# Values of a batch's tokens from seven block products in place of eight, in a decoder layer on one core

## The chip, the core and the metric

The kernel runs on one core of a Trainium2 chip, as one program with one launch. The metric is the device time of that program in microseconds: the median of several runs. Of the engines, TensorE (PE in the profile, its weight loads PEld) multiplies matrices, VectorE (DVE), ScalarE (ACT) and GpSimd (POOL) work element by element, and SyncE (SP) issues most of the DMAs. Each engine works through a queue of its own in a fixed order. [...]

## The reference

A decoder layer in fp32 over 16 batches of 256 tokens with 256 features. Each of three parts is added to its input and layer-normed.

```python
x = layernorm(x + recurrent(x))              # in-projection, causal convolution, 16-state scan, out-projection
x = layernorm(x + cross_attention(ctx, x))   # 8 heads of 128
x = layernorm(x + experts(x))                # 8 experts, top 2, capacity 512 tokens each
```

The second part matters here. Its keys and values come from the 77 normed context rows and from the 256 normed tokens of the same batch (333 rows in all), its queries from the tokens:

```python
xn = _layernorm(ctx, gamma_media, beta_media)
ln = _layernorm(x, gamma_lat, beta_lat)
q = ln @ Wq + bq
kv = concatenate([xn, ln], axis=1) @ Wkv + bkv
k, v = split(kv, 2, axis=-1)
out = softmax(q k^T * DH**-0.5) v            # per head
return out @ Wo + bo
```

The values of a batch's tokens, before the bias, are a matrix of 256 tokens by 1024 columns: the product of a 256 x 256 matrix (tokens by features) with a 256 x 1024 matrix (the right half of `Wkv`).

## The kernel before

**Stages.** A prologue runs the recurrent part for the first pair of batches and makes the normed context (`context`), its values for all batches (stored in DRAM as `vc`) and everything that batch 0 needs. Then comes the head loop: 16 batches x 8 heads. It ends at about 1066 us, and the experts follow to the end at 1230 us.

**The head loop.** Iteration i issues `head_kq` of head i (keys `pk`, queries `pq`), then extra steps that hang on this head, then `head_out` of head i-2 (values times probabilities, `po`), `head_softmax` of head i (scores `s` on TensorE; `nm` on DVE, exponentials on ACT, `rs` and `pn` on DVE) and `head_turn` of head i-1 (transposes `pa`, `pb`, copied to `ptt`).

**The extra steps.** A dictionary `steps`, filled through `at(b, h, f, ...)`, says which piece of other work stands at which head of which batch: finishing batch b-1 (`project` with `pw`, `turn_tokens`, `score_experts` with `pl`, `choose`, `dispatch`, `settle`) and preparing batch nb = b+1. Even batches prepare an odd one and also run the in-projections (`rec_in`, `ph`) of the next pair at heads 4 to 7; odd batches prepare an even one, with `rec_state` and `rec_out` first. Preparing a batch means `prep_norm` (`zl`), `prep_keys` (the transposed normed tokens `kvt`, one half of the features at a time) and `prep_values`.

**The values.** `prep_values(b, n)` is called for n = 0 to 3, at heads 4, 5, 6, 7 of odd batches and 1, 4, 5, 6 of even ones. Call n takes one block of 128 tokens (`jc`) and one half of the 1024 columns (`half`): two products with 128 features each, accumulated in one bank `pv`, which DVE (half 0) or ACT (half 1) copies into `vs[b]`. Call 0 also issues the DMA that brings the context's values (`v<-vc`). A matmul of fp32 numbers that is written once appears in the trace as two instructions.

**Banks.** `pk`, `pq`, `pa`, `po` have a bank each and `s` two. The remaining two have the tag `mm` and serve all extra steps, the values among them.

**Order.** The program framework (`TileContext`) places waits by itself, and for each engine makes the order in which its instructions are put into its queue when the program is built: among instructions that it thinks ready, by its own estimates of costs, the one written first. Once built, the order of a queue is fixed.

Of the kernel before, what the change touches and what calls it, by code (L numbers as in the profile page):

```python
# [10 lines left out]
F32 = mybir.dt.float32  # L11
I32 = mybir.dt.int32
AF = mybir.ActivationFunctionType
ALU = mybir.AluOpType
# [4 lines left out]
P = 128  # L19
# [9 lines left out]
INNER = H * DH  # L29
E, FI, CAP = 8, 512, N // 8  # L30
DC = D // P
# [7 lines left out]
def decoder_layer(  # L39
# [29 lines left out]
    V, A, G, T = nc.vector, nc.scalar, nc.gpsimd, nc.tensor  # L69
# [14 lines left out]
    def bank(name, tag="mm", bufs=2):  # L84
        return ps.tile([P, 512], F32, tag=tag, bufs=bufs, name=name)
# [79 lines left out]
    wpool = work.enter_context(tc.tile_pool(name="wB", bufs=1))  # L165
# [5 lines left out]
    wkv_s = wpool.tile([P, DC, 2 * INNER], F32, tag="wkv", name="wkv_s")  # L171
# [6 lines left out]
    gl = wpool.tile([P, DC], F32, tag="gl", name="gl")  # L178
    bl = wpool.tile([P, DC], F32, tag="bl", name="bl")
    emb_s = wpool.tile([P, DC, E], F32, tag="emb", name="emb_s")  # L180

    kvc = wpool.tile([P, DC, B * M], F32, tag="kvc", name="kvc")

    b2 = work.enter_context(tc.tile_pool(name="b2", bufs=2))
    b1 = work.enter_context(tc.tile_pool(name="b1", bufs=1))
# [27 lines left out]
    for t0, t1 in ((0, 1), (1, 5), (5, NCT - 1), (NCT - 1, NCT)):  # L213
        c = b2.tile([P, t1 - t0, D], F32, tag="v" if t1 - t0 == 4 else "ctx", name=f"ctx{t0}")
# [104 lines left out]
    def rec_out(b):  # L319

        pr, i = divmod(b, PB)
        py = bank(f"py{b}")
        for h in range(2):
            c0 = i * S + h * P
            T.matmul(py[:, h * D : (h + 1) * D], lhsT=yss[pr][:, c0 : c0 + P], rhs=outw, start=True, stop=True)
        y = b2.tile([P, 2, D], F32, tag="ya", name=f"ya{b}")
        V.tensor_tensor(
            y.rearrange("p h d -> p (h d)"),
            py,
            xts.pop(b).rearrange("p h d -> p (h d)"),  # L330
            ALU.add,
        )
        xs[b] = xpool.tile([P, 2, DX], F32, tag="xs", name=f"xs{b}")
        stats[b] = layernorm(xs[b], y, 2, P, f"a{b}")
        if b + 2 < B:
            load_x(b + 2)
# [3 lines left out]
    zs, kvts, vs, outs_t = {}, {}, {}, {}  # L340
# [47 lines left out]
    def prep_keys(b):  # L388
# [12 lines left out]
            )  # L401
        kvts[b] = kvt

    def prep_values(b, n):

        if n == 0:
            vs[b] = b2.tile([P, 3, INNER], F32, tag="v", name=f"v{b}")
            nc.sync.dma_start(vs[b][0:M, 2, :], vc_d[b * M : (b + 1) * M, :])
        jc, half = divmod(n, 2)
        pv = bank(f"pv{b}_{n}")  # L410
        f0 = half * 512
        for k in range(DC):
            T.matmul(  # L413
                pv,
                lhsT=kvts[b][:, k, jc * P : (jc + 1) * P],
                rhs=wkv_s[:, k, INNER + f0 : INNER + f0 + 512],
                start=(k == 0),
                stop=(k == DC - 1),
            )
        if half == 0:  # L420
            V.tensor_copy(vs[b][:, jc, f0 : f0 + 512], pv)
        else:
            A.copy(vs[b][:, jc, f0 : f0 + 512], pv)

    kts, qts, pns, ptts = {}, {}, {}, {}

    def head_kq(b, h):

# [233 lines left out]
    def at(b, h, f, *args):  # L662
        if 0 <= b < B:
            steps[b, h].append((f, args))
# [4 lines left out]
    for b in range(B):  # L669
        nb = b + 1  # L670
        new_pair = nb % PB == 0 and nb < B
        if b > 0:
            early = int(b == B - 1)
            at(b, 2, project, b - 1, 0)
            at(b, 3, project, b - 1, 1)
            at(b, 5 - early, turn_tokens, b - 1)
            at(b, 6 - early, score_experts, b - 1)
            at(b, 6 - early, choose, b - 1)
            at(b, 7 - early, dispatch, b - 1)
            at(b, 7, settle, b - 1)  # L680
        if new_pair:
            at(b, 0, rec_state, nb // PB)
            at(b, 1, rec_out, nb)
            at(b, 2, prep_norm, nb)
            at(b, 3, rec_out, nb + 1)
            at(b, 3, prep_keys, nb)
            for n, h in enumerate((4, 5, 6, 7)):
                at(b, h, prep_values, nb, n)
        elif nb < B:
            at(b, 0, prep_norm, nb)  # L690
            at(b, 0, prep_keys, nb)
            for n, h in enumerate((1, 4, 5, 6)):
                at(b, h, prep_values, nb, n)
            if nb + 1 < B:
                pr = (nb + 1) // PB
                at(b, 0, load_xT, pr)
                for c in range(NI):
                    at(b, 4 + c, rec_in, pr, c)
# [12 lines left out]
    prep_keys(0)  # L711
    context(4)
    rec_out(1)
    for n in range(4):
        prep_values(0, n)
    for t in range(5, NCT):
        context(t)
# [248 lines left out]
```

## Time and profile before

| | us |
|---|---|
| median of 3 runs | 1229.26 (1229.24 to 1230.31) |
| profiled execution | 1232.08 |
| its span (first to last instruction) | 1230.4 |
| PE busy (matmuls) | 1187.3 (96%) |
| DVE busy | 725.9 (59%) |
| ACT busy | 489.4 (40%) |
| POOL busy | 274.5 (22%) |
| value products of the batches (L413, 256 instructions) | 121.6 busy, of 592 ns each (median) |
| their copies on DVE (L421, 32) | 22.0, of 688 ns each |
| their copies on ACT (L423, 32) | 18.7, of 585 ns each |

How to read it: a line such as `L413 PE MATMUL pv<-wkv_s,kvt` names the source line, the engine, the operation, and the tiles written and read. Durations of matmuls contain the time in which results still drain while the next matmul already streams, so the busy time of neighbours overlaps, and the distance between starts is the better measure of what a matmul costs. In a row of groups the mean duration is followed by the idle time of the engine before it and by what ended it. A timeline row has the start, the time from the first start to the last end, and the number of instructions that follow each other.

### The profile page before, as it was taken

How to read it: one execution, taken by the hardware profiler on the slowest of the kernel's cores; microseconds unless marked ns; L12 is line 12 of the kernel's file. 1: busy time of each engine (PE TensorE's matmuls, PEld its weight loads, DVE VectorE, ACT ScalarE, POOL GpSimd, SP SyncE). 2: the span in 40 equal slices, each digit the busy share in tenths (PEclk: the TensorE clock that was granted, in tenths of full speed). 3: DMA queues.
4: the chain of work that ended last, by engine and by line, in shares of the span. 5: the costliest groups of instructions: out<-in, count | busy, mean ns of one | idle time of the engine just before them, and what ended most of it. 6: DMA issues, size and time to landing. Idle time of an engine off the chain costs nothing.

```text
span 1230.4 us, 15284 instructions
## 1 busy us (share of the span) xinstructions
PE 1187.3 (96%) x5000; PEld 842.3 (68%) x5000; DVE 725.9 (59%) x2122; ACT 489.4 (40%) x1270; POOL 274.5 (22%) x500
## 2 busy tenths in 40 slices
PE   7799999999999999999999999999999999889995
PEld 3356777767776777677767776777677778756663
DVE  6535755684558555756486548564766464555654
ACT  3135434443435344534353434443543344313331
POOL 3200021122111311131111210221021112135566
PEclk9899999999999999999999999999999999999998
DMA  8730100010001100010000000000001000146762
GB/s 262 245 107 1 37 18 29 9 54 18 29 9 32 37 11 20 26 37 5 19 21 28 12 19 19 22 9 14 9 13 43 13 9 3 29 146 147 177 158 82
DMA packets 43617, 60.80 MB, mean 49 GB/s; under 512 B 7945, under 2 KB 31414, under 8 KB 43538
## 3 DMA queue, kind: packets, MB, share of 16 engines
q1 hardware_dynamic: 36674, 50.34, 12.8%
q0 software_dynamic: 6144, 9.48, 3.3%
q8 instruction: 39, 0.64, 0.2%
q14 instruction: 40, 0.33, 0.1%
q10 hardware_dynamic: 720, 0.01, 0.0%
HBM read 36.55 MB, written 30.78 MB: 55 GB/s over the span
## 4 chain that ended last, share of the span: by engine, by line
PE 82%; DVE 7%; POOL 3%; issue 3%; DMA 3%; ACT 1%; POOLq 0%; SPq 0%; DVEq 0%
PE po L484 12%; PE pk L433 10%; PE s L448 10%; PE pw L502 9%; PE pq L438 8%; PE pv L413 8%; PE ph L281 5%; PE pa L471 4%; PE pi L798 3%; PE pvc L365 3%; PE px L301 2%; PE pf L814 2%; PE pb L471 2%; PE pl L544 1%; DMA xe<-xg 1%
## 5 line engine op out<-in xcount | busy, mean ns | idle before, releaser
L450 DVE TENSOR_REDUCE nm<-s 128x2 f32<-128x666 f32 x128 | 108.4, 847 | 144.7 <-PE s L448 144.4
L484 PE MATMUL po<-ptt,v 128*128 128x256 f32 (+1 forms) x768 | 190.2, 382 | 2.2 <-DVE ptt L473 2.2
L484 PEld LDWEIGHTS po<-ptt,v 128*128 128x128 f32 (+1 forms) x768 | 144.2, 191 | 57.1 <-issue 32.7
L433 PE MATMUL pk<-kvt,wkv_s 128*128 128x333 f32 x512 | 165.1, 444 | 0.0
L448 PE MATMUL s<-kt,qt 128*128 128x333 f32 x512 | 164.4, 442 | 0.0
L492 ACT ACTIVATE ot<-po,bkv_s 128x256 f32<-128x256 f32 x128 | 60.6, 474 | 235.4 <-PE po L484 235.3
L454 ACT ACTIVATE p<-s,nm 128x333 f32<-128x333 f32 x256 | 135.1, 534 | 37.9 <-DVE nm L450 28.6
L438 PE MATMUL pq<-kvt,wq_s 128*128 128x256 f32 x512 | 131.2, 379 | 0.0
L413 PE MATMUL pv<-wkv_s,kvt 128*128 128x512 f32 x256 | 121.6, 599 | 0.0
L448 PEld LDWEIGHTS s<-kt,qt 128*128 128x128 f32 x512 | 96.5, 189 | 31.2 <-ACT qt L440 0.5
L438 PEld LDWEIGHTS pq<-kvt,wq_s 128*128 128x128 f32 x512 | 96.7, 189 | 30.5 <-issue 0.5
L474 ACT COPY ptt<-pb 77x256 f32<-77x256 f32 x128 | 47.1, 368 | 177.3 <-PE pb L471 175.9
L502 PE MATMUL pw<-wo_s,ot 128*128 128x256 f32 x512 | 117.2, 381 | 0.0
L502 PEld LDWEIGHTS pw<-wo_s,ot 128*128 128x128 f32 x512 | 97.4, 191 | 13.4 <-ACT ot L492 0.2
L433 PEld LDWEIGHTS pk<-kvt,wkv_s 128*128 128x128 f32 x512 | 87.6, 191 | 23.0
L459 DVE TENSOR_SCALAR pn<-p,rs 128x333 f32<-128x333 f32 x256 | 93.1, 397 | 4.2
L471 PEld LDWEIGHTS pa<-ident,pn 128*128 128x128 f32 x512 | 63.5, 141 | 38.7 <-DVE pn L459 11.1
L649 POOL DMA_INDIRECT xg<-xs,sidx x64 | 67.3, 1052 | 93.1 <-DVE sidx L646 78.4
L473 DVE COPY ptt<-pa 128x512 f32<-128x512 f32 x128 | 87.3, 682 | 0.9 <-PE pa L471 0.6
L513 POOL TENSOR_TENSOR xb<-xs,bo_s 128x256 f32<-128x256 f32 x32 | 21.2, 684 | 283.4 <-DVE yb L515 283.4
L471 PE MATMUL pa<-ident,pn 128*128 128x128 f32 x512 | 78.8, 274 | 5.9 <-DVE pn L459 5.9
L290 DVE SCALAR_TENSOR_TENSOR cv<-hp,cw,cv 128x512 f32<-128x512 f32 x96 | 71.4, 749 | 2.0
(167 smaller groups left out, 1596.4 us busy)
## 6 DMA issues: line engine op xcount, KB each, us to landing
v<-vc SPq DMA_DIRECT2D x16, 308.0 KB
vc<-vc SPq DMA_DIRECT2D x9, 512.0 KB
xg<-zero SPq DMA_DIRECT2D x17, 262.0 KB
xe<-xg SPq DMA_DIRECT2D x8, 524.0 KB
xT<-in_xT SPq DMA_DIRECT2D x8, 512.0 KB
xt<-in_x_in SPq DMA_DIRECT2D x16, 256.0 KB
out<-o SPq DMA_DIRECT2D x16, 256.0 KB
w<-in_w1T SPq DMA_DIRECT2D x8, 512.0 KB
```

The source lines that it names most:

```text
L290: V.scalar_tensor_tensor(cv, hp[:, :, k : k + S], cw[:, c, k : k + 1], cv, ALU.mult, ALU.add)
L413: T.matmul(pv, lhsT=kvts[b][:, k, jc * P : (jc + 1) * P], rhs=wkv_s[:, k, INNER + f0 : INNER + f0 + 512], start=(k == 0), stop=(k == DC - 1),)
L433: T.matmul(pk[:, 0:J], lhsT=wkv_s[:, k, f], rhs=kvt[:, k, :], start=(k == 0), stop=(k == DC - 1))
L438: T.matmul(pq[:, 0:S], lhsT=wq_s[:, k, f], rhs=kvt[:, k, 0:S], start=(k == 0), stop=(k == DC - 1))
L448: T.matmul(s[:, ic, 0:J], lhsT=qt[:, ic * P : (ic + 1) * P], rhs=kt, start=True, stop=True)
L450: V.tensor_reduce(nm, s[:, :, 0:J], AX.X, ALU.max, negate=True)
L454: A.activation(p[:, ic, :], s[:, ic, 0:J], AF.Exp, bias=nm[:, ic : ic + 1], accum_out=sm[:, ic : ic + 1])
L459: V.tensor_scalar(pn[:, ic, :], p[:, ic, :], rs[:, ic : ic + 1], None, ALU.mult)
L471: T.transpose(dst[0:jn, c0 : c0 + P], pn[:, ic, j0 : j0 + jn], ident)
L473: V.tensor_copy(ptt[:, 0:2, :], pt01.rearrange("p (j i) -> p j i", j=2))
L484: T.matmul(po[:, 0:S], lhsT=vs[b][0:jn, jc, h * DH : (h + 1) * DH], rhs=ptt[0:jn, jc, :], start=(jc == 0), stop=(jc == 2),)
L502: T.matmul(pws[b][:, i * D : (i + 1) * D], lhsT=ot[:, h, i * P : (i + 1) * P], rhs=wo_s[:, h, :], start=(h == 0), stop=(h == H - 1),)
```

## The change

The tokens' matrix is cut into four blocks of 128 x 128 (token block by feature half), and the value weights into four of 128 x 512. Winograd's form of Strassen's scheme gives the four blocks of the result from seven products of sums of blocks. The four sums of weight blocks are made once, on DVE in the prologue (`weight_sums`, kept in `wsum`). The four sums of token blocks are made for each batch on POOL after `prep_keys` (`prep_sums`). `prep_values` has three calls per batch. The first makes products 1 and 6 in two banks, has ACT copy product 1 out, adds product 6 on DVE, then adds product 2 to product 1 in its bank and has ACT copy that out. The second makes product 5, which DVE adds to the result so far, then adds product 3 in the same bank, and DVE adds again. The third does the same with products 7 and 4. The calls stand at heads 4, 6, 7 of odd batches and at 1, 4, 6 of even ones.

```diff
+    wsum = wpool.tile([P, 4, 512], F32, tag="wsum", name="wsum")
...
+    def weight_sums():
+        w = lambda k, half: wkv_s[:, k, INNER + half * 512 : INNER + (half + 1) * 512]
+        t = lambda i: wsum[:, i, :]
+        V.tensor_tensor(t(0), w(0, 1), w(0, 0), ALU.subtract)
+        V.tensor_tensor(t(1), w(1, 1), w(0, 1), ALU.subtract)
+        V.tensor_tensor(t(2), w(1, 1), t(0), ALU.subtract)
+        V.tensor_tensor(t(3), w(1, 0), t(2), ALU.subtract)
+        return w(0, 0), w(1, 0), w(1, 1), t(3), t(0), t(2), t(1)
+    def prep_sums(b):
+        x = lambda i, k: kvts[b][:, k, i * P : (i + 1) * P]
+        sums = b1.tile([P, 4, P], F32, tag="tsum", name=f"tsum{b}")
+        s = lambda i: sums[:, i, :]
+        G.tensor_tensor(s(0), x(1, 0), x(1, 1), ALU.add)
+        G.tensor_tensor(s(2), x(0, 0), x(1, 0), ALU.subtract)
+        G.tensor_tensor(s(1), s(0), x(0, 0), ALU.subtract)
+        G.tensor_tensor(s(3), x(0, 1), s(1), ALU.subtract)
+        tsums[b] = x(0, 0), x(0, 1), s(3), x(1, 1), s(0), s(1), s(2)
     def prep_values(b, n):
...
-        jc, half = divmod(n, 2)
-        pv = bank(f"pv{b}_{n}")
-        f0 = half * 512
-        for k in range(DC):
-            T.matmul(
-                pv,
-                lhsT=kvts[b][:, k, jc * P : (jc + 1) * P],
-                rhs=wkv_s[:, k, INNER + f0 : INNER + f0 + 512],
-                start=(k == 0),
-                stop=(k == DC - 1),
-            )
-        if half == 0:
-            V.tensor_copy(vs[b][:, jc, f0 : f0 + 512], pv)
+        def product(dst, i, more):
+            T.matmul(dst, lhsT=tsums[b][i - 1], rhs=wparts[i - 1], start=not more, stop=True, skip_group_check=True)
+        c = lambda i, half: vs[b][:, i, half * 512 : (half + 1) * 512]
+        if n == 0:
+            p1, p6 = bank(f"pv1{b}"), bank(f"pv6{b}")
+            product(p1, 1, False)
+            product(p6, 6, False)
+            A.copy(c(1, 0), p1)
+            V.tensor_tensor(c(1, 0), c(1, 0), p6, ALU.add)
+            product(p1, 2, True)
+            A.copy(c(0, 0), p1)
+        elif n == 1:
+            p5 = bank(f"pv5{b}")
+            product(p5, 5, False)
+            V.tensor_tensor(c(1, 1), c(1, 0), p5, ALU.add)
+            product(p5, 3, True)
+            V.tensor_tensor(c(0, 1), c(1, 0), p5, ALU.add)
         else:
-            A.copy(vs[b][:, jc, f0 : f0 + 512], pv)
+            p7 = bank(f"pv7{b}")
+            product(p7, 7, False)
+            V.tensor_tensor(c(1, 1), c(1, 1), p7, ALU.add)
+            product(p7, 4, True)
+            V.tensor_tensor(c(1, 0), c(1, 0), p7, ALU.add)
...
             at(b, 3, rec_out, nb + 1)
             at(b, 3, prep_keys, nb)
-            for n, h in enumerate((4, 5, 6, 7)):
+            at(b, 3, prep_sums, nb)
+            for n, h in enumerate((4, 6, 7)):
                 at(b, h, prep_values, nb, n)
         elif nb < B:
             at(b, 0, prep_norm, nb)
             at(b, 0, prep_keys, nb)
-            for n, h in enumerate((1, 4, 5, 6)):
+            at(b, 0, prep_sums, nb)
+            for n, h in enumerate((1, 4, 6)):
                 at(b, h, prep_values, nb, n)
...
     rec_out(1)
-    for n in range(4):
+    wparts = weight_sums()
+    prep_sums(0)
+    for n in range(3):
         prep_values(0, n)
```

More of the change, by code (lines that the diff above doesn't have):

```diff
@@ L408, in prep_values @@
             nc.sync.dma_start(vs[b][0:M, 2, :], vc_d[b * M : (b + 1) * M, :])
-        jc, half = divmod(n, 2)
-        pv = bank(f"pv{b}_{n}")
-        f0 = half * 512
-        for k in range(DC):
-            T.matmul(
-                pv,
-                lhsT=kvts[b][:, k, jc * P : (jc + 1) * P],
-                rhs=wkv_s[:, k, INNER + f0 : INNER + f0 + 512],
-                start=(k == 0),
-                stop=(k == DC - 1),
-            )
-        if half == 0:
-            V.tensor_copy(vs[b][:, jc, f0 : f0 + 512], pv)
-        else:
-            A.copy(vs[b][:, jc, f0 : f0 + 512], pv)
-    kts, qts, pns, ptts = {}, {}, {}, {}
+        def product(dst, i, more):
[15 more added lines that the diff above has]
+            V.tensor_tensor(c(0, 1), c(1, 0), p5, ALU.add)
+        else:
+            p7 = bank(f"pv7{b}")
[3 more added lines that the diff above has]
+            V.tensor_tensor(c(1, 0), c(1, 0), p7, ALU.add)
+    kts, qts, pns, ptts, tsums = {}, {}, {}, {}, {}
     def head_kq(b, h):
```

## The prediction, made before the changed kernel was run

> **What bounds the kernel now.** I first read the busy time by stage. Each row has the stretch, its length, then busy time and instruction count of PE, PEld, DVE, ACT, POOL, the granted clock, and DMA.
>
> ```profile
> core 0: us, PE busy (x) PEld busy (x) DVE busy (x) ACT busy (x) POOL busy (x), PEclk, DMA share, GB/s
> 100.00:500.00 400.00, 397.93 (x1724) 287.86 (x1723) 244.26 (x647) 172.63 (x462) 65.58 (x139) 1.00 0.07 23
> 500.00:1066.00 566.00, 563.62 (x2496) 415.52 (x2496) 344.40 (x994) 242.23 (x658) 103.63 (x197) 1.00 0.06 18
> ```
>
> The head loop (about 77 to 1066 us) is TensorE's: idle for 2.07 of 400 us and 2.38 of 566 us, at full clock. DVE is at 61%, ACT at 43%. A busy PE need not be a PE at its peak, so I looked at start times in the timeline of one head where the value products stand:
>
> ```profile
> 421.68 0.81 PE L438 MATMUL pq<-kvt,wq_s 128*128 128x256 f32 x3
> 422.33 1.88 PE L413 MATMUL pv<-wkv_s,kvt 128*128 128x512 f32 x4
> 424.04 1.46 PE L484 MATMUL po<-ptt,v 128*128 128x256 f32 x6
> 425.34 1.28 PE L448 MATMUL s<-kt,qt 128*128 128x333 f32 x4
> 427.00 0.63 PE L471 MATMUL pa<-ident,pn 128*128 128x128 f32 x2 [0.37 <-DVE pn L459]
> ```
>
> Groups overlap by about 0.16 us (each row's end lies past the next one's start): they stream without a hole. The value group takes 424.04 - 422.33 = 1.71 us for four instructions, so 0.427 us each. One written matmul with 512 columns shows as two instructions, so **a product costs TensorE 0.855 us**. The last row shows one of the rare holes: a transpose waits for DVE's `pn`.
>
> Next, who decides the order on TensorE. This is its timeline where the head loop begins:
>
> ```profile
> 82.77 0.73 PE L433 MATMUL pk<-kvt,wkv_s 128*128 128x333 f32 x2
> 83.34 1.28 PE L448 MATMUL s<-kt,qt 128*128 128x333 f32 x4
> 84.46 0.72 PE L433 MATMUL pk<-kvt,wkv_s 128*128 128x333 f32 x2
> 85.02 1.02 PE L438 MATMUL pq<-kvt,wq_s 128*128 128x256 f32 x4
> ```
>
> In the code, the scores `s` of head 0 stand ahead of all of head 1's `pk`. In the trace two of `pk`'s four instructions run before them. So the order is not the written one: the framework's planner puts another ready matmul where, by its own estimates, an operand would be late. The new products bring waits into TensorE's stream, so this matters most here.
>
> **The change, part by part.** The profiled execution took 1232.08 us (span 1230.4 and 1.7 around it), 2.8 above the median of 1229.26; I sum against the first and carry the difference over.
>
> *Removed: one product of eight.* Four groups of two products a batch become seven products: 16 batches x 0.855 = **-13.7 us**, nearly all on a saturated TensorE, so all of it shortens the end unless something else gets late.
>
> *Waits added.* Three times a batch a bank is read between two products and then added to. Product 2 waits for ACT's copy of bank `p1`, product 3 for DVE's addition from `p5`, product 4 for that from `p7`. Lengths: an addition of 128x512 with one operand in PSUM is the row of L515, 0.692 us, and ACT's copy that of L423, 0.585.
>
> ```profile
> L515 DVE TENSOR_TENSOR yb<-pw,xb 128x512 f32<-128x512 f32 x16 | 11.1, 692 | 54.1 <-PE pw L502 54.1
> L423 ACT COPY v<-pv 128x512 f32<-128x512 f32 x32 | 18.7, 585 | 42.2 <-PE pv L413 42.2
> L513 POOL TENSOR_TENSOR xb<-xs,bo_s 128x256 f32<-128x256 f32 x32 | 21.2, 684 | 283.4 <-DVE yb L515 283.4
> ```
>
> With a drain of 0.16 us (the overlap above) and about 0.2 us for two handovers (at 440.06 the DVE copy starts 0.19 us after `pv`'s modelled end at 439.87), an uncovered DVE wait costs 0.16 + 0.2 + 0.69 = 1.05 us. For product 2, product 6 streams meanwhile: 0.16 + 0.2 + 0.585 - 0.855 leaves 0.1 us, more if ACT is late. All uncovered: 32 x 1.05 + 16 x 0.1 = 35 us. All covered: 0. Here a rule of the Trainium skill speaks against the change. "TensorE: Matmul & The Clock Gate", "Step-by-step: what each phase is for", says that only weight loads are pulled ahead and that "the MATMULs themselves stay in program order". Whatever stands behind product 3, `po` and `s` of the running head included, then stands too, and the sum is -13.7 + 35 = +21 us. The rows at 82.77 to 85.02 do not deny the rule; they show that the order given to the chip already has other matmuls where a wait was foreseen. Ready work is at hand in each of these heads: `po` with 1.28 us of streaming, `s` with 1.11, and in half of the cases a `ph` group with 1.71. I go by the row. What is left is the planner's error. A matmul is 0.2 to 0.43 us long and holes elsewhere in the loop are rare, so I take 0.1 us for each of the 48 waits: **+4.8 us**, with 0 and 35 as ends.
>
> *DVE.* Per batch two copies (0.69) become five additions (0.692): +2.1 us, 33 us in all, 726 to 759 of 1230. On average it lies beside TensorE. It is tightest in even batches, heads 5 to 7:
>
> ```profile
> 487.80:497.00 9.20, 9.20 (x39) 5.92 (x38) 6.91 (x14) 3.99 (x10) 0.10 (x1) 1.00 0.00 1
> 497.00:506.30 9.30, 9.30 (x42) 6.35 (x41) 8.20 (x29) 4.78 (x12) 0.10 (x1) 1.00 0.01 2
> 506.30:513.60 7.30, 7.30 (x35) 5.31 (x34) 7.11 (x26) 3.99 (x10) 1.72 (x3) 1.00 0.24 67
> ```
>
> Head 6 holds the choice of experts and a convolution. Its DVE goes from 8.20 to 9.6 of 9.3 us, and head 5 loses a copy (6.91 to 6.2) and its product (9.2 to 7.5). Over these three DVE does 22.9 us of work against 24.1 of TensorE: not yet the bound, and `pn` has a whole head to arrive. I take 0, and 2 us for each of seven batches as the upper end.
>
> *ACT* keeps two copies a batch, now both beside the first group: 0.
>
> *POOL: four sums of 128x128 a batch.* Between L513 (256 columns, 684 ns) and the 2-column L154 (196 ns, median) a straight line gives 0.44 us each, 1.8 us a batch, 28 in all on an engine with 274 busy. In even batches POOL is idle there (head 0). In odd ones they meet a chain that TensorE already waits on:
>
> ```profile
> 423.31 0.16 DVE L456 RECIPROCAL rs<-sm 128x2 f32<-128x2 f32 x1
> 426.28 0.35 DVE L385 TENSOR_SCALAR zl<-xs,rlz 128x256 f32<-128x256 f32 x1 [2.82 <-POOL rlz L132]
> 426.55 0.69 DVE L459 TENSOR_SCALAR pn<-p,rs 128x333 f32<-128x333 f32 x2
> ```
>
> `pn` could have run at 423.5 but stands in DVE's queue behind `zl`, which waits for POOL's `rlz`; this is the 0.37 us hole at 427.00, 0.54 counted from the end of streaming. The sums come into POOL's queue ahead of that chain. If they go into its idle 1.78 us before `ra` (421.93), `ra` moves by 0.7 us at most, and product 2 gives TensorE 0.855 more to do first: the hole stays about as it is. If all are in front of `rlz`, the hole grows by 1.8 - 0.86, about 0.9, over seven odd batches +6.6; if the planner turns `pn` and `zl` round, -3.8. I take 0.
>
> *Once:* four differences of 128x512 on DVE with both operands in SBUF. The nearest rows are L290 and L294 (749 and 700 ns), so 2.8 us. DVE waits 3.9 us before its copy at 49.00, and the values are not begun until 52.81: 0, at most 2.8. The first batch's POOL sums start after `kvt` (45.07) and end by 47.
>
> *Moved:* the groups stand at heads 4, 6, 7 (odd batches) and 1, 4, 6 (even) in place of 4 to 7 and 1, 4, 5, 6. The first group keeps its head, and with it the load `v<-vc`; SP's queue is passed by nothing. POOL's sums stand after `kvt` and ahead of the products, past no scatter. The first group now holds both banks of tag `mm`. In even batches it holds them until `po` of the batch before has freed `v` (DVE's copy waits for that now, until 460.72); the next user, `pw`, comes at 464.3, so 0; uncovered, one addition per batch, 0.7 x 8 = 5.5.
>
> Sum: 1232.1 - 13.7 + 4.8 = 1223.2 for a profiled execution, and **1220.4** by the median.
>
> **The rivals.**
> 1. *Main forecast:* waits filled. With none of the 4.8 and the `pn` hole gone 1212; with 0.2 us for each wait 1225. Chance 0.62.
> 2. *A late queue gives most of it back:* the sums in front of `rlz` (+6.6) with DVE behind in even batches (7 x 0.5 = 3.5) on top of 4.8: 1229.3 - 13.7 + 14.9 = 1230.5; with either alone, 1224 to 1227. For it: `pn` behind `zl` shows that the planner thinks POOL faster than it is. Against: TensorE has 0.86 more work in just that head. Chance 0.24, some half of it still faster.
> 3. *TensorE stands at products 3 and 4* (and a little at 2), because the planner leaves them where they are written or thinks the additions much earlier than they are. Up to +21, so 1250. It decides against the change from 13.7 / 48 = 0.28 us a wait. For it: the additions share DVE with 18 chained small operations of the choice (439 to 442). Against: in that same chain a value copy now starts within 0.2 us of its product's end. Chance 0.14.
> That the eighth product isn't saved is no rival: seven calls stand in the diff.
>
> **How the numbers follow.** The prediction is the first case's 1220.4. A range from 1213 to 1230.5 leaves out the best end of case 1, and nearly all of case 3. About 0.2% (2.5 us) is what a measurement can tell from no change. Faster by more: nearly all of case 1 and half of case 2, with a little of 3, 0.76. Within it: most of the rest of case 2, 0.09. Slower: 0.15.
>
> **What would show it.** Products in groups that take 0.855 us each and 13.7 us less busy streaming in all; `po`, `s` or `ph` between products 5 and 3 and between 7 and 4; the PE's idle time before the value products about 5 us; DVE near 759 us and POOL near 300; the hole before `pa` in odd batches between 0 and 1.5 us. I am wrong if products 3 and 4 follow 5 and 7 directly with a hole of about 1 us (case 3), or if the idle time before `pa` or `po` grows by more than 8 us (case 2).

## The result, and the profile after

| | before | after |
|---|---|---|
| median of 5 runs, us | 1230.28 (1229.24 to 1230.93) | 1224.28 (1222.53 to 1224.49) |
| profiled execution, us | 1232.08 | 1224.40 |

The ratio is 0.9949 [0.9935, 0.9964]: 6.0 us faster between the medians (7.7 between the profiled executions), less than half of the 13.7 that the missing products were to give. The forecast was 1220.4.

The busy line of the page after, with busy time, share of the span and instructions of each engine:

```profile
PE 1174.4 (96%) x4968; PEld 835.6 (68%) x4968; DVE 754.1 (62%) x2174; ACT 487.4 (40%) x1270; POOL 304.8 (25%) x564
```

PE is busy for 12.9 us less than before (1187.3), DVE for 28 us more, POOL for 30 us more. Two stretches of the head loop (length, busy time of PE, PEld, DVE, ACT, POOL, granted clock, DMA); before the change PE was busy for 397.93 us of the first and for 552.62 of the second:

```profile
100.00:500.00 400.00, 395.90 (x1722) 287.04 (x1721) 259.31 (x686) 172.18 (x463) 76.91 (x163) 1.00 0.07 23
500.00:1055.00 555.00, 549.56 (x2452) 407.25 (x2451) 352.25 (x998) 238.18 (x650) 117.84 (x229) 1.00 0.06 18
```

PE is now idle for 4.1 and 5.4 us where it was idle for 2.1 and 2.4. DVE has risen to 65% of the first stretch, far from full, and the granted clock is 1.00 as before. So part of the saving came back as idle time of TensorE.

The length of the head loop is the cleanest measure in what follows: the first and the last start of the scores `s`. In the answer for tile `s` (minimum, median and maximum duration in ns, then the two starts), before:

```profile
L448 PE MATMUL s<-kt,qt x512: 441/442/504, 83.3 to 1063.3; 128*128 128x333 f32 x171
```

and after:

```profile
L486 PE MATMUL s<-kt,qt x512: 441/442/507, 82.5 to 1055.4; 128*128 128x333 f32 x171
```

The loop went from 980.0 to 972.9 us, 7.1 less. Fifteen of the sixteen batches get their values inside it, so the missing products are worth 15 x 0.855 = 12.8 us there. The waits of PE before and after show where the rest is. The columns are the idle time in us, the number of waits, and the longest one. Before:

```profile
PE pa L471 <- DVE pn L459: 5.9, 7, 3.6
```

After:

```profile
PE pv L438 <- DVE v L452: 4.0, 7, 0.6
PE pa L509 <- DVE pn L497: 3.5, 1, 3.5
PE pv L438 <- ACT v L445: 3.3, 7, 0.5
PE po L522 <- DVE ptt L511: 2.2, 7, 0.3
```

Two kinds of wait are new in the loop, each in seven batches: product 3 waits for DVE's addition (L452), product 2 for ACT's copy (L445). One is gone: of the waits for `pn` only the single long one outside the loop is left. The wait for `ptt` was there before.

**Product 2.** PE's timeline in head 4 of the odd batch that the prediction showed (start, length, instructions, idle time before and what ended it):

```profile
419.00 1.02 PE L438 MATMUL pv<-wkv_s,kvt 128*128 128x512 f32 x2
419.86 1.02 PE L438 MATMUL pv<-wsum,tsum 128*128 128x512 f32 x2
421.36 1.12 PE L438 MATMUL pv<-wkv_s,kvt 128*128 128x512 f32 x2 [0.48 <-ACT v L445]
422.32 1.46 PE L522 MATMUL po<-ptt,v 128*128 128x256 f32 x6
423.62 1.28 PE L486 MATMUL s<-kt,qt 128*128 128x333 f32 x4
424.74 0.47 PE L509 MATMUL pa<-ident,pn 128*128 128x128 f32 x2
```

Products 1, 6 and 2 follow each other directly, with `po` and `s` behind them. Product 6 has streamed out at 419.86 + 0.855 = 420.72, and product 2 starts at 421.36: a hole of 0.64 us, of which the row shows 0.48 since it subtracts the drain. ACT's timeline says why:

```profile
419.93 0.54 ACT L473 ACTIVATE kt<-pk,bkv_s 128x333 f32<-128x333 f32 x1
420.35 0.48 ACT L478 ACTIVATE qt<-pq,bqs 128x256 f32<-128x256 f32 x1
420.71 0.60 ACT L445 COPY v<-pv 128x512 f32<-128x512 f32 x1
```

Product 1 has ended at 419.00 + 1.02 = 420.02, but ACT's copy stands in its queue behind `kt` and `qt` of the running head and starts at 420.71. It ends at 421.31, and product 2 starts 0.05 later. The copy is not long; its place in the queue is late.

**Product 3.** PE in head 4 of an even batch:

```profile
478.04 1.02 PE L438 MATMUL pv<-wsum,tsum 128*128 128x512 f32 x2
478.90 1.02 PE L282 MATMUL ph<-xT,inw 128*128 128x512 f32 x2
480.49 1.10 PE L438 MATMUL pv<-wkv_s,tsum 128*128 128x512 f32 x2 [0.58 <-DVE v L452]
481.43 1.02 PE L282 MATMUL ph<-xT,inw 128*128 128x512 f32 x2
```

Between product 5 and product 3 the planner has put half of a `ph` group, 0.855 us of streaming; the other half comes behind product 3. DVE at the same time:

```profile
478.86 0.17 DVE L494 RECIPROCAL rs<-sm 128x2 f32<-128x2 f32 x1 [0.62 <-ACT p L492]
479.06 0.70 DVE L497 TENSOR_SCALAR pn<-p,rs 128x333 f32<-128x333 f32 x2
479.67 0.68 DVE L452 TENSOR_TENSOR v<-v,pv 128x512 f32<-128x512 f32 x1
```

The addition (0.68 us, as forecast) could have begun at about 479.06, when product 5 had drained. It stands behind `pn`, and `pn` behind `rs`, which waited for ACT. So it ends at 480.35, and TensorE stands from 479.76 to 480.49, 0.74 us. Six even batches look like this. In batch 14, which has no `ph`, the fill is four of the six `po` instructions, 0.86 us, and the hole 0.73; in batch 0 it is only 0.18.

**Product 4** shows how it looks when the fill is enough. PE in head 7 of an odd batch:

```profile
441.01 1.10 PE L438 MATMUL pv<-wsum,tsum 128*128 128x512 f32 x2
441.95 1.46 PE L522 MATMUL po<-ptt,v 128*128 128x256 f32 x6
443.25 1.02 PE L438 MATMUL pv<-wsum,kvt 128*128 128x512 f32 x2
```

`po` lies between products 7 and 4 with 1.30 us from start to start, and there is no hole.

**What a hole costs.** More than its length, since what follows it starts slowly. The group after a product that waited begins 0.96 us (421.36 to 422.32) or 0.94 us later (480.49 to 481.43), where 0.855 is the rule. With the old hole before `pa` this is larger. PE's timeline before the change, one head without that hole and the next with it:

```profile
165.14 0.60 PE L471 MATMUL pa<-ident,pn 128*128 128x128 f32 x4
165.58 0.38 PE L471 MATMUL pb<-ident,pn 128*77 128x128 f32 x2
...
172.46 0.85 PE L471 MATMUL pa<-ident,pn 128*128 128x128 f32 x4 [0.38 <-DVE pn L459]
173.15 0.38 PE L471 MATMUL pb<-ident,pn 128*77 128x128 f32 x2
```

The same four transposes take 0.69 us to the next start in place of 0.44. So a hole before `pa` of 0.54 cost 0.54 + 0.25 = 0.79 us, one before product 2 costs 0.64 + 0.10 = 0.74, one before product 3 0.74 + 0.09 = 0.83. A slow start does not need a hole, though: in a seventh odd head of the kernel before (935.54) the transposes take 0.69 us with no hole in front of them, and in six of its even batches a value group and the `ph` group behind it (235.71 and 237.52) take 1.81 and 1.82 us in place of 1.71.

**The balance of the loop**, from the distances between all of TensorE's starts in the two traces: 12.8 for the products, less 11.3 at the value products (7 x 0.74 = 5.2 for product 2, 7 x 0.83 = 5.8 for product 3, 0.3 in the first two batches), plus 4.4 at `pa` (3.2 for the six old holes that are gone, and 1.2 because the slow starts of seven heads shrink from 0.25 to 0.08 us), plus 1.2 because the six `ph` groups behind value products no longer start slowly: 7.1, as measured.

### The profile page after: what moved, and what is told of

It reads as the page before. It is cut to its first block, busy times and chain, and to the rows that moved or that the text cites. A ratio compares the mean times of both kernels' runs of the same rounds, so it can differ in the third digit from the quotient of the medians.

```text
span 1222.7 us, 15361 instructions
## 1 busy us (share of the span) xinstructions
PE 1174.4 (96%) x4968; PEld 835.6 (68%) x4968; DVE 754.1 (62%) x2174; ACT 487.4 (40%) x1270; POOL 304.8 (25%) x564
## 3 DMA queue, kind: packets, MB, share of 16 engines
q1 hardware_dynamic: 36674, 50.34, 12.8%
## 4 chain that ended last, share of the span: by engine, by line
PE 74%; DVE 9%; DMA 3%; issue 3%; POOL 2%; ACT 2%; POOLq 0%; ACTq 0%; DVEq 0%
PE po L522 12%; PE pk L471 10%; PE s L486 10%; PE pw L540 9%; PE pq L476 8%; PE pv L438 6%; PE pa L509 4%; PE ph L282 4%; PE pb L509 2%; PE px L302 2%; DMA ge<-oe,at 2%; PE pi L840 1%; PE py L326 1%; DVE nm L488 1%; PE pl L582 1%
## 5 line engine op out<-in xcount | busy, mean ns | idle before, releaser
L282 PE MATMUL ph<-xT,inw 128*128 128x512 f32 x128 | 64.8, 616 | 6.9 <-DMA xT<-in_xT 6.3
```

What stands on the lines that cost most here:

```text
L282: T.matmul(ph, lhsT=inw[:, k, c * P : (c + 1) * P], rhs=xTs[pr][:, k, :], start=(k == 0), stop=(k == DC - 1))
```

## The experiments

The theory was that the removed products count in full, and that three holes decide the rest: product 2 behind ACT's queue, product 3 behind DVE's, and the hole of `pn`, which POOL's sums would widen if product 2 did not stand in front of it. The rivals were that the missing product itself is worth less than 0.855 us, that DVE's extra work costs time by its amount, and that the new waits as such (48 of them) cost something. Loop lengths are read from the scores as above; each experiment was compared with the kernel before on the same chip.

| experiment | median, us | ratio to before | head loop, us |
|---|---|---|---|
| before | | 1 | 980.0 |
| after | 1224.28 | 0.9949 [0.9935, 0.9964] | 972.9 |
| e1_seven_plain | 1219.02 | 0.9909 [0.9896, 0.9921] | 967.5 |
| e2_dve_more | 1231.45 | 1.0011 [1.0003, 1.0019] | 980.1 |
| e3_pool_sums | 1235.24 | 1.0044 [1.0032, 1.0056] | 986.2 |
| e4_as_written | 1219.84 | 0.9922 [0.9909, 0.9934] | 971.0 |
| e5_p2_later | 1229.60 | 0.9991 [0.9983, 1.0] | 978.2 |
| e6_p3_behind_ph | 1217.43 | 0.9898 [0.9883, 0.9913] | 967.5 |
| e9_all_behind | 1254.89 | 1.0199 [1.0185, 1.0213] | 1003.5 |
| e12_both_zl | 1213.64 | 0.9863 [0.9848, 0.9878] | 961.9 |
| e13_zl_only | 1224.56 | 0.9930 [0.9911, 0.9948] | 972.2 |
| e14_before_zl | 1226.62 | 0.9947 [0.9929, 0.9965] | 975.0 |

The kernel before took 1230.22 us beside e1 to e4, 1230.05 beside e5 to e12, and 1233.34 beside e13 and e14.

**e1_seven_plain: only one product fewer.** The kernel before, without the second product of the last block.

```diff
-        for k in range(DC):
+        nk = DC - 1 if n == 3 else DC
+        for k in range(nk):
...
-                stop=(k == DC - 1),
+                stop=(k == nk - 1),
```

> The kernel before with the last of a batch's eight value products left out (its fourth value group sums over half of the features only), and nothing else of the change: no additions, no sums, no waits. Theory A (TensorE's saving is worth its full 13.7 us, and the 6 us measured are what the new waits leave of it): 13 to 14 us below before, about 1216.5, and the holes before the transposes as before. Rival B (the saving itself is partly off the path, so that even without waits a head gets late elsewhere): 6 to 9 us below before.

Measured: 11.2 us faster, short of the 13 to 14 expected of the whole time, but the loop is 12.5 shorter against 12.8 for the fifteen products in it. The holes before `pa` stayed. A product that is simply not there is worth its streaming time; the saving is on the path. The 1.3 us that the whole time falls short of the loop's gain lie outside the loop, and no run here says why.

**e2_dve_more: only DVE's work.** The kernel before, with one addition more after each of calls 1 to 3, out of the bank (the `[128, 512]` tile in PSUM that the product was written to).

```diff
+        if n > 0:
+            extra = b2.tile([P, 512], F32, tag="extra", name=f"extra{b}_{n}")
+            V.tensor_tensor(extra, kvts[b].rearrange("p k j -> p (k j)")[:, 0:512], pv, ALU.add)
```

> The kernel before with three extra additions of 128x512 a batch on DVE, each reading a value bank and writing a scratch tile: the change's load on DVE (48 x 0.69 = 33 us) without its waits on TensorE. Theory A (DVE's extra work lies beside TensorE): within 2 us of before. Rival B (DVE's load is what takes 7 us of the 13.7): 4 to 10 us slower than before.

Measured: 1.2 us slower in all, the loop 0.1 longer, with DVE busy for 753.9 us, as much as after the change. DVE's amount of work costs the loop nothing.

**e3_pool_sums: only POOL's sums.** The kernel before with `prep_sums`, whose results nobody reads.

```diff
+            at(b, 3, prep_sums, nb)
...
+            at(b, 0, prep_sums, nb)
...
```

> The kernel before with the four sums of token blocks a batch on POOL, unused: the change's load on POOL alone. Theory A (the sums cost nothing, and the 0.5 us holes before the transposes in odd batches went away in the changed kernel because product 2 gave TensorE more to do first): within 1 us of before, and these holes still there, 0.3 to 1.3 us each. Rival B (the sums in POOL's queue make the planner turn pn and zl round, and that took the holes away): 3 to 4 us faster than before, no holes. Rival C (the sums hold up ra and rlz): 2 to 7 us slower.

Measured: 5.0 us slower, the loop 6.2 longer: rival C, and not the theory. DVE's timeline of this kernel in the odd head:

```profile
428.81 0.35 DVE L385 TENSOR_SCALAR zl<-xs,rlz 128x256 f32<-128x256 f32 x1 [2.83 <-POOL rlz L132]
429.07 0.69 DVE L469 TENSOR_SCALAR pn<-p,rs 128x333 f32<-128x333 f32 x2
```

and PE's:

```profile
426.96 1.28 PE L458 MATMUL s<-kt,qt 128*128 128x333 f32 x4
429.52 0.74 PE L481 MATMUL pa<-ident,pn 128*128 128x128 f32 x3 [1.27 <-DVE pn L469]
```

The scores stream for 1.12 us, so the hole before `pa` has grown from 0.54 to 429.52 - 426.96 - 1.12 = 1.44 us in six batches, and in a seventh, which started slowly already, a hole of 0.9 is new: 7 x 0.9 = 6.3, the whole of the loop's loss. Four small sums on an engine that is a quarter busy cost 5 us, because they stand in POOL's queue ahead of the chain `ra`, `rlz`, on which DVE's queue (`zl`, then `pn`) waits. In the changed kernel POOL's timeline has them in that very place (the last of the four is shown):

```profile
419.08 0.45 POOL L424 TENSOR_TENSOR tsum<-kvt,tsum 128x128 f32<-128x128 f32 x1
419.49 0.70 POOL L132 TENSOR_TENSOR ra<-va,nhalf 128x2 f32<-128x2 f32 x1
```

and on DVE `pn` stands behind `zl` there as well:

```profile
423.87 0.35 DVE L386 TENSOR_SCALAR zl<-xs,rlz 128x256 f32<-128x256 f32 x1 [2.84 <-POOL rlz L132]
424.14 0.69 DVE L497 TENSOR_SCALAR pn<-p,rs 128x333 f32<-128x333 f32 x2
```

Yet TensorE comes to `pa` only at 424.74, and the hole is gone. Product 2 and its own hole give TensorE 0.855 + 0.64 = 1.5 us before it reaches `pa`, more than the 1.44 that `pn` is late.

**e5_p2_later: the hole of product 2 taken away.** The changed kernel with product 2 one head later in odd batches, so that ACT has long copied.

```diff
+        elif n == "2":
+            p1 = p1s.pop(b)
             product(p1, 2, True)
             A.copy(c(0, 0), p1)
...
-            for n, h in enumerate((4, 6, 7)):
+            for n, h in ((0, 4), ("2", 5), (1, 6), (2, 7)):
...
```

> The changed kernel with product 2 of odd batches written one head later (head 5, which has no product), so that TensorE no longer waits for ACT's copy: seven holes of 0.64 us go. Theory A (POOL's sums have moved rlz, and with it zl and pn, later by 0.9 us, as the run with the sums alone shows; product 2 and its hole only hide that): the holes before the transposes of head 3 come back with 1.2 to 1.4 us each, and it is 4 to 6 us slower than the changed kernel, about 1229. Rival B (the two holes have nothing to do with each other): 4.5 us faster, about 1219.5.

Measured: 1229.60, some 5.3 us slower than the changed kernel, though seven holes of 0.64 are gone. PE's timeline in the odd head:

```profile
421.81 1.02 PE L438 MATMUL pv<-wsum,tsum 128*128 128x512 f32 x2
422.67 1.46 PE L526 MATMUL po<-ptt,v 128*128 128x256 f32 x6
423.97 1.28 PE L490 MATMUL s<-kt,qt 128*128 128x333 f32 x4
426.51 0.85 PE L513 MATMUL pa<-ident,pn 128*128 128x128 f32 x4 [1.25 <-DVE pn L501]
```

The hole before `pa` is there with 426.51 - 423.97 - 1.12 = 1.42 us, as in e3. The two are in series in front of the same late `pn`. Six such holes at 1.42 and one of 0.87 are 9.4 us; slow starts add 1.2; less the seven holes of product 2 at 0.74, that is 5.4 us, and the loop is 5.3 longer. Taking away the shorter stall bares the longer one.

**e6_p3_behind_ph: the hole of product 3 taken away.** The changed kernel with product 3 written behind the whole `ph` group (four instructions) of the head.

```diff
...
                     at(b, 4 + c, rec_in, pr, c)
+                    if c == 0:
+                        at(b, 4, prep_values, nb, "3")
...
```

> The changed kernel with product 3 of even batches written behind the in-projection ph of the same head, so that four matmuls (1.71 us) stand between products 5 and 3 in place of two (0.85). Theory A (the wait is 1.45 us long because DVE's addition stands behind pn, which comes late; the planner put too little in between): the seven holes of 0.74 us go, about 5 us faster than the changed kernel, about 1219. Rival B (the hole moves to another place in the head, since DVE is what is late there): within 1.5 us of the changed kernel.

Measured: 1217.43, with the loop 5.4 us shorter than after the change. Of the seven waits for L452, one is left:

```profile
PE pv L438 <- DVE v L452: 0.6, 1, 0.6
```

The one left is in batch 14, which has no `ph` to put in between. Six at 0.83 are 5.0 of the 5.4 us. The median fell by 6.9; what lies outside the loop is not settled.

**e4_as_written and e9_all_behind: what an unfilled wait costs.** e4 was to show the price of waits with nothing between the products: everything that is written behind products 3 and 4 in the same head was ordered behind them.

```diff
+        with tc.issue_after(last[0]) if last and i < len(heads) else ExitStack():
+            if i >= 2:
+                head_out(*heads[i - 2])
...
```

> The changed kernel, but what is written behind products 3 and 4 in their heads (ph, po, s, the transposes) is kept behind them on TensorE, so that nothing fills these two waits. Theory A (an uncovered wait costs about 1.05 us, and the planner's filling is what makes the change pay): 30 waits in the loop at 1.05 less the 5.4 us that product 3 already loses, 26 us slower than the changed kernel, about 1250; 20 slower than before. Rival B (TensorE has slack further on that takes a stand of 1 us back): less than 10 us slower than the changed kernel.

Measured: 1219.84, faster than the changed kernel by 4.4 us (the loop by 1.9). It did not take the fill away. PE's timeline in an odd head:

```profile
432.99 1.10 PE L438 MATMUL pv<-wsum,tsum 128*128 128x512 f32 x2
433.93 1.29 PE L474 MATMUL pk<-kvt,wkv_s 128*128 128x333 f32 x4
435.06 1.02 PE L438 MATMUL pv<-wkv_s,tsum 128*128 128x512 f32 x2
```

The planner took `pk` of the next head, 1.13 us, which was not ordered. Product 3's seven waits are gone, and seven of `pk` for `kt`, 1.7 us by PE's list of waits, stand in their place. So this run says nothing on an unfilled wait. In e9 the next heads are ordered behind the products too.

```diff
...
+            with behind():
+                head_kq(*heads[i])
...
+                with behind():
+                    f(*args)
...
```

> As e4_as_written, but the next head's keys and queries and all that follows are kept behind products 3 and 4 too; in e4 the planner had taken the next head's pk (1.11 us) to fill the waits. Now product 3 follows 5, and 4 follows 7, with nothing between. Theory A (an uncovered wait costs TensorE its whole length): 30 waits of 1.0 to 1.4 us, less the 5.4 that product 3 loses in the changed kernel: 25 to 36 us slower than the changed kernel, about 1249 to 1260. Rival B (a stand of TensorE is made good later in the head): less than 12 us slower than the changed kernel.

Measured: 1254.89, 30.6 us slower than the changed kernel, all of it in the loop. Product 4 in an odd batch:

```profile
452.40 1.10 PE L438 MATMUL pv<-wsum,tsum 128*128 128x512 f32 x2
454.28 1.12 PE L438 MATMUL pv<-wsum,kvt 128*128 128x512 f32 x2 [0.78 <-DVE v L460]
```

and product 3 in an even one:

```profile
490.48 1.02 PE L438 MATMUL pv<-wsum,tsum 128*128 128x512 f32 x2
492.94 1.10 PE L438 MATMUL pv<-wkv_s,tsum 128*128 128x512 f32 x2 [1.44 <-DVE v L454]
```

The second starts 2.46 us after the first; less 0.855 that is a hole of 1.6. Over the loop such holes are 0.94 to 1.6 us long, 1.14 on average, and TensorE runs nothing in them although `ph`, `po` and `s` are ready and merely queued behind. This is the rule of the Trainium skill that the prediction weighed ("TensorE: Matmul & The Clock Gate", "Step-by-step: what each phase is for"): it holds, and with it the same arithmetic is 25 us slower than the kernel before. The order in the queue is what makes the change a gain.

**e13_zl_only and e14_before_zl: the hole of `pn` by itself.** The third hole can be removed by turning `pn` and `zl` round in DVE's queue: `prep_norm` is ordered behind the last `pn` of head 4. e13 does this in the changed kernel, e14 in the one before.

```diff
+    def norm_behind(b):
+        with tc.issue_after(pn_last[b - 2, 4]) if b > 1 else ExitStack():
+            prep_norm(b)
...
...
-            at(b, 0, prep_norm, nb)
+            at(b, 0, norm_behind, nb)
```

> The changed kernel with only DVE's zl for the batch after next put behind pn of head 4 (in odd batches), products as they are. Theory A (in the changed kernel product 2 and its hole already cover what POOL's chain holds up, so taking that chain away alone gains nothing): within 1 us of the changed kernel, about 1224, with the holes at products 2 and 3 as there. Rival B (the chain costs time in other places too): 3 us or more faster than the changed kernel.

Measured: 1224.56. The kernel before took 3.1 us more beside it than beside the changed kernel, so the loop decides: it is 0.7 shorter than after the change, and the waits at products 2 and 3 are those of the changed kernel. In the changed kernel `pn` is no longer what TensorE waits for.

> The kernel before with the same order of zl behind pn, and nothing of the change. Theory A (what the best version gains over before is the seven products' 12.8 us in the loop and this order's 3.8 us): 3.5 to 4.5 us faster than before, the holes of 0.54 us before the transposes gone. Rival B (the order gains nothing by itself, and the whole 16 us of the best version are the products'): within 1 us of before.

Measured: 6.7 us faster than the kernel before beside it (1233.34 in that set); that is more than the 3.5 to 4.5 expected. The loop is 5.0 shorter: the six holes before `pa`, 3.2 us, are gone, and so are the slow starts of seven heads, 1.7. The other 1.7 us of the median lie outside the loop and are not explained. The same edit brings 5.0 us of loop where the hole is open and 0.7 where another hole lies over it.

**e12_both_zl: all three at once.** Product 2 later as in e5, product 3 behind `ph` as in e6, `zl` behind `pn` as in e13.

> The changed kernel with product 2 one head later in odd batches, product 3 behind ph in even ones, and DVE's zl for the batch after next put behind pn of head 4, so that POOL's rlz holds up no pn. Theory A (the three holes are all that the change loses in the loop): all gone, 9.5 to 10.5 us faster than the changed kernel, about 1214. Rival B (with DVE at 62% and its queue in a fixed order, new holes open elsewhere): 1218 or more.

Measured: 1213.64 us (1213.05 to 1214.51), the fastest of all: 16.4 below the kernel before beside it and 10.6 below the changed one. PE in the even head:

```profile
474.79 1.02 PE L444 MATMUL pv<-wsum,tsum 128*128 128x512 f32 x2
475.64 1.88 PE L282 MATMUL ph<-xT,inw 128*128 128x512 f32 x4
477.36 1.02 PE L444 MATMUL pv<-wkv_s,tsum 128*128 128x512 f32 x2
```

DVE in the odd head:

```profile
423.07 0.17 DVE L507 RECIPROCAL rs<-sm 128x2 f32<-128x2 f32 x1 [0.70 <-ACT p L505]
423.27 0.69 DVE L510 TENSOR_SCALAR pn<-p,rs 128x333 f32<-128x333 f32 x2
423.88 0.61 DVE L386 TENSOR_SCALAR zl<-xs,rlz 128x256 f32<-128x256 f32 x2
```

The four `ph` instructions give 1.72 us from start to start, and product 3 follows without a hole, six times out of seven. `pn` runs right after `rs`, and `zl` comes after it. Against e14, which has the same order of `zl` but eight products, the loop is 975.0 - 961.9 = 13.1 us shorter, against 12.8 for fifteen products (less one hole that is left in batch 14). With the holes out of the way, the seven products bring all that they should.

## Why the prediction came out as it did

The direction held, and the mechanism in part: removed products count in full and the planner fills most waits, but what the waits cost sits in a few holes and not in a little at each. The result lies in the main case's own span of 1212 to 1225, 3.9 us above its point. Made against the profiled execution the sum said 1223.2, and 1224.4 was measured; most of the 3.9 is that the profiled execution before lay 2.8 us above the median of its runs, and that after only 0.1. Larger errors in opposite directions stand behind the small one; that they nearly cancel is luck.

1. *Products, -13.7.* Right. e1 shows the loop's share in full (12.5 of 12.8), e12 against e14 as well.
2. *Waits, +4.8 as 48 x 0.1.* The step that failed. The holes in the loop cost 11.3 us, and one in the prologue 0.5 (0.34 in its row and the drain). In PE's list of waits 7.3 us stand before the loop's value products, where about 5 had been named as the sign. An average per wait was the wrong form: 14 of the waits cost 0.74 or 0.83 each, and nearly all the others nothing. The planner did fill, with `ph` or `po`, as the rows on `pk` had suggested. But it put 0.855 us where about 1.6 were needed, because the reading instruction stood behind others that were late. What the planner had assumed of DVE and ACT is not on record. Whether the fill is enough could have been asked from the profile before, by the place of the copies in the queues of DVE and ACT.
3. *Product 2, "0.1 us, more if ACT is late".* ACT was late: `kt` and `qt` stand ahead of the copy, and the hole is 0.64.
4. *The `pn` hole, "stays about as it is", 0.* Wrong by -4.4. POOL's sums moved the chain by 0.9 us (e3), where 0.7 was taken as the most. But product 2 gave TensorE not only its 0.855 us but its own hole too, and 1.5 us cover all that `pn` is late. The hole was priced with product 2's streaming and without product 2's own hole, though the two lie one behind the other in front of the same late result. The rival of `pn` and `zl` turned round was priced at -3.8 and brings 5.0 in the loop (e14), since it also ends seven slow starts.
5. *DVE, 0.* Right (e2: 0.1 us in the loop); its busy time came to 754.1 against 759. *POOL's sums:* 0.41 to 0.46 us each as worked out (0.44), POOL 304.8 against 302. *ACT's amount of work, 0:* right (489.4 to 487.4 us busy); the place of its copy is error 3. *The moved groups, the weight sums, 0:* no new wait of TensorE inside the loop names them. Not foreseen are the 1.2 us of `ph` groups that no longer start slowly.
6. *"As the code is written", 1250.* The price per wait, 1.05, and its place were about right: e9 gives holes of 1.14 on average and 1254.9. The given order decided against it, as argued from the timeline.

Put together with the measured terms: 1232.1 - 13.7 + 11.3 + 0.5 - 4.4 - 1.2 = 1224.6, against 1224.4.

## What to carry to other kernels

On an engine that is saturated and works in order, as TensorE is here, removed work counts in full (e1, e12), but each wait put in its place counts as the shortfall of what stands between: for every such wait, look up which instruction makes the result, which instructions stand ahead of that one in its own queue, and how late those are, and then compare with the streaming time of the fill (0.855 us was too little here, 1.30 and 1.72 were enough). Stalls in series in front of one late result hide each other, so removing one alone can make things slower (e5) or do next to nothing (e13), while removing all pays in full (e12). A little work on an idle engine is not free when it stands ahead of a chain on which a busier engine's queue waits (e3).

## What the runs showed of the hardware that was not expected

- Four POOL instructions a batch of 0.41 to 0.46 us each, on an engine that was 22% busy, lengthened the loop by 6.2 us through two other queues (POOL's `rlz`, DVE's `zl` and `pn`, then TensorE).
- TensorE starts slowly after a hole, and in some places without one: four transposes took 0.69 us in place of 0.44, a product 0.94 to 0.96 in place of 0.855. With this the balances of the loop come out to within 0.3 us. What takes the time is not settled.
- The rest of the span, outside the loop, varied by 4.2 us between profiled executions of kernels with the same work there: 246.7 us in e4 and 250.9 in e12. The granted clock differs with it, 0.96 before and 0.95 behind the loop in e4, 0.94 and 0.94 in e12, against 1.00 inside the loop in both. That the clock is the cause was not tested, and it may not be the whole of it; small differences were read from the loop for this reason.
